# Attention pairs of a conv network: transposes re-ordered against scores and projection, 3x3 taps of two strips started earlier, one group norm of the next layer moved

## The chip, the core and the metric

The kernel runs on one core of one Trainium2 chip. A core has five engines that run side by side and wait for each other by semaphores: TensorE (PE in the profile: matmuls and, with an identity as one operand, transposes), VectorE (DVE), ScalarE (ACT), GpSimd (POOL) and SyncE (SP, which here issues the DMAs). Each engine takes its own instructions in the order in which the program has written them. The metric is the device time in microseconds of the whole launch, four images long; the median of three runs is the number that counts. Beside it there is one execution under the hardware profiler, whose span and instructions are what the profile shows.

## The reference, cut to what matters

Four images of 256 channels by 64 by 64 pass through four pre-normed layers. The change touches the first two, which are the same function with different weights:

```python
def layer(x):                       # layers 0 and 1, x: (b, 256, 64, 64)
    xn = group_norm(x)              # each pair of columns by its mean and variance over channels, rows
    y  = mhsa(xn)                   # tanh/sigmoid gates, a scan along the image: gives y
    q, k, v = split(windows(y) @ qkv_w.T + qkv_b)       # 64 windows of 8 x 8 tokens
    idx = top_k(mean(q) @ mean(k).T, 4)                 # routing: 4 windows for each window
    kg, vg = k[idx], v[idx]                             # gather: 256 keys and values
    a   = softmax(q * SCALE @ kg.T) per head            # 8 heads of 32 channels
    out = a @ vg
    out = out + depthwise_conv3x3(v_img, lepe_w) + lepe_b
    return x + out @ wo_w.T + wo_b
```

The work is cut into eight strips of 8 columns of the image; a strip holds four of the norm's groups, so its statistics need that strip only. Layers 2 and 3 are state-space layers, which the change leaves alone.

## The kernel before, in words

The four images are processed one after the other by unrolled code; each goes through attention layer 0, attention layer 1 and then the two state-space layers. An attention layer has three stages.

**Scan stage** (`scan_phase`). Eight strips. For strip s it computes the gates, the scan, and, one strip late, `keys_values(s - 1)`: the V and K projections on PE, V written by ACT into the image buffer `vimg` (L357), a copy on POOL into window order (`vst`, L361), eight transposes into `vt`, copies `vn` by DVE and ACT (L389, L390) and the DMAs of K and V to DRAM. The 3x3 depthwise convolution ("taps", made by `lepe`) of strip s - 3 is done on DVE between these. `lepe(lay, s, ...)` returns the steps of strip s: for each half m of the channels nine taps. On DVE a tap is one instruction (`step`); on POOL the first is one and every other is two (`weigh` into the one buffer `tap`, then `add` into `vimg`), so that a half is 9 steps on DVE and 17 on POOL. `[:9]` is half 0 with DVE's steps, `[17:]` half 1 with POOL's. The buffer of `weigh` has the tag `sq`, one buffer, which the squares of the group norm (`gn_sq`) share.

**Routing stage** (`routing`, and the lines after it in `attention_layers`). The means, the logits, the top four; then the queries of strips 2 to 4, with nine DVE taps between them and 17 POOL taps behind them, both of strip 5.

**Window stage** (`window_phase`). 32 iterations of one pair of windows each, i = 4 sj + a. The heads are cut in two parities, h = 0 and 1. For each pair and parity:

- `scores(i, h)`: 32 small matmuls into `sc`, one buffer for each parity; needs the gathered keys and the exponentials of the previous pair out of that buffer.
- `smallest(i, h)`: the reduction `mn` on DVE (L550).
- `exps(i, h, part)`: four exponentials on ACT (L561), in two parts.
- `normalise(i, h)`: the reciprocal `sm` on DVE (L573) and four multiplications of `pr` on POOL (L576).
- `turn(i, h)`: eight transposes on PE (L589) into two buffers `pt`, which both parities share.
- `turned(h, j)`: the copies `pts` out of `pt`, j = 0 by DVE (L600), j = 1 by ACT (L602).
- `values(i)`: 64 small matmuls (L615), once for each pair; `own_rows(i)` (L626) adds them into `vimg`.

Beside these an iteration may hold one convolution on PE (L232): `project(sj - 1, a - 1)` for a = 1, 2 (output projection; its result is added to `x` by DVE at L636, the call `add()` at the end of the iteration) and the late queries of strips 6 and 7 for a = 3 and a = 0 from i = 19 on (their result is written by ACT, `evict()`, also at the end). These convolutions and the small statistic matmuls of the norms share one PSUM buffer, tag `mm`. POOL taps of strip 6 (half 1) and strip 7 (both halves) are put two to an iteration, one behind each `normalise`; DVE taps of strip 6 (half 0) one to an iteration from i = 2 to 10. Group norms of the next layer's strips 0 and 1 (layer 0), or the statistics for layer 2 (layer 1), are put into iterations by `plan`: a list `mids`, run ahead of `normalise(i, 0)`, and a list `ends`, run at the end of the iteration. A norm has seven steps: sums (DVE), a matmul for the mean, center (DVE copy and a POOL subtraction, L151), square (ACT, L156), reduce (DVE), a matmul for the variance, scale (POOL power L168 and multiplication L172).

The order of work is written out by hand; nothing reorders it. Thus the order on PE around the change is, before, for an iteration with a convolution: scores(i, 1), turn(i-1, 1), convolution, scores(i+1, 0), values(i-1), turn(i, 0), the statistic matmul if there is one, scores(i+1, 1), and so on.

Of the kernel before, what the change touches and what calls it, by code (L numbers as in the profile page):

```python
# [23 lines left out]
NW = 8  # L24
# [20 lines left out]
class Net:  # L45
# [33 lines left out]
    def attention_layers(self, x, w_drams, v_drams):  # L79
        tc, nc = self.tc, self.nc  # L80
        with ExitStack() as ctx:
# [235 lines left out]
            def scan_phase(lay, work, psum, tail):  # L317
# [78 lines left out]
                for s in range(NW):  # L396
                    g = gn_four(lay, s + 2, lambda: psum) if s + 2 < NW else [lambda: None] * 4
                    taps = lepe(lay, s - 3, psum) if s >= 3 else []
                    g[0]()
                    xn = lay["xn"].pop(s).rearrange("p c w h -> p c (w h)")  # L400
                    ha, ha_half = hidden("ha", W1A, xn, AF.Tanh, vec[:, B1A : B1A + 2])
                    hb, hb_half = hidden("hb", W1B, xn, AF.Tanh, vec[:, B1B : B1B + 2])
                    z, z_half = hidden("z", W2A, ha, AF.Tanh, vec[:, B2A : B2A + 2])

                    f, f_half = hidden("f", W2B, hb, AF.Tanh, lay["half_b2b"], scale=0.5)
                    for half in (ha_half, hb_half):
                        half(0)
                        half(1)
                    for t in taps[:9]:
                        t()  # L410
                    if s == 0:
                        for t in tail:
                            t()
                        load_attention_weights(lay)
                    g[1]()
                    z_half(0)
                    z_half(1)
                    for t in taps[9:]:
                        t()
                    g[2]()  # L420
                    f_half(0)
                    f_half(1)
                    scan(s, f, z)
                    if s:
                        keys_values(s - 1)
                    g[3]()
                    if s >= 6:
                        double(s - 6)
                    if s in (5, 6):
                        for evict in [query(lay, s - 5, m, psum) for m in range(2)]:  # L430
                            evict()
                keys_values(NW - 1)


            def routing(lay, work, psum):
# [30 lines left out]

            def window_phase(lay, work, psum, idx, nxt):
                vec, wb = lay["vec"], lay["wb"]  # L470
                n_pair = NW * NW // 2
                regs, kv, pr, sm, ov = {}, {}, {}, {}, {}
# [125 lines left out]
                def turned(h, j):  # L598
                    if j == 0:
                        nc.vector.tensor_copy(pts[h][0], pt[h][0])  # L600
                    else:
                        nc.scalar.activation(pts[h][1], pt[h][1], AF.Copy)  # L602
# [47 lines left out]
                early = [query(lay, 5, m, psum, nc.vector, tag="pt", bufs=2) for m in range(2)]  # L650
                smallest(0, 0)
                smallest(0, 1)
                taps6, taps7 = (lepe(lay, s, pool=True) for s in (NW - 2, NW - 1))
                taps = taps6[17:] + taps7[17:] + taps7[:17]
                dve_taps = lepe(lay, NW - 2)[:9]

                mids, ends, left = {}, {}, []

                def plan(steps, *where):
                    for f, (at, i) in zip(steps, where):  # L660
                        if i < n_pair:
                            at.setdefault(i, []).append(f)
                        else:
                            left.append(f)

                if nxt:
                    load_scan_weights(nxt)
                    for s in range(2):
                        i = 10 + s
                        plan(gn(nxt, s, lambda: psum), (ends, i), (ends, i + 1), (mids, i + 2),  # L670
                             (ends, i + 2), (mids, i + 3), (ends, i + 5), (mids, i + 6))
                else:

                    for s in range(NW - 1):
                        i = 4 * s + 6
                        last = i + 6 if s < 5 else i + 3
                        plan(stats(s, lambda: psum), (ends, i), (ends, i + 1), (mids, i + 2),
                             (ends, i + 2), (ends, last), (mids, last + 1))
                for i in range(n_pair):
                    sj, a = divmod(i, 4)  # L680
                    add = evict = None
                    exps(i, 0, (0, 1))
                    if i:
                        scores(i, 1)
                        turned(0, 0)
                        turned(0, 1)
                        turn(i - 1, 1)
                        smallest(i, 1)
                    exps(i, 0, (2, 3))
                    for t in mids.get(i, ()):  # L690
                        t()
                    if i == 0:
                        for f in early:
                            f()
                    normalise(i, 0)
                    for t in taps[2 * i : 2 * i + 1]:
                        t()
                    if a == 3 and sj + 2 in (NW - 2, NW - 1):
                        evict = query(lay, sj + 2, 0, psum)
                    elif a == 0 and sj + 1 in (NW - 2, NW - 1):  # L700
                        evict = query(lay, sj + 1, 1, psum)
                    elif a in (1, 2) and sj:
                        add = project(sj - 1, a - 1, psum)
                    exps(i, 1, (0, 1))
                    scores(i + 1, 0)
                    if i:
                        turned(1, 0)
                        turned(1, 1)
                        values(i - 1)
                    turn(i, 0)  # L710
                    smallest(i + 1, 0)
                    exps(i, 1, (2, 3))
                    normalise(i, 1)
                    if i:
                        own_rows(i - 1)
                    for t in taps[2 * i + 1 : 2 * i + 2]:
                        t()
                    for t in dve_taps[i - 2 : i - 1] if i > 1 else ():
                        t()
                    if add:  # L720
                        add()
                    if evict:
                        evict()
                    gather(i + 3)
                    if a == 0 and 1 < sj + 1 < NW - 2:
                        double(sj + 1)
                    elif a == 1 and sj + 1 in (NW - 2, NW - 1):
                        double(sj + 1)
                    indices(i + 4)
                    for t in ends.get(i, ()):  # L730
                        t()
                turned(0, 0)
                turned(0, 1)
                turn(n_pair - 1, 1)
                turned(1, 0)
                turned(1, 1)
                values(n_pair - 1)

                def tail(m):
# [17 lines left out]
            for i, lay in enumerate(layers):  # L757
                with tc.tile_pool(name=f"at_a{i}", bufs=1, reuse_waits="tile") as work, tc.tile_pool(
                    name=f"at_p{i}", bufs=5, space=PSUM, reuse_waits="tile"
                ) as psum:  # L760
                    box["psum"] = psum
                    scan_phase(lay, work, psum, tail)
                    idx = routing(lay, work, psum)
                    taps = lepe(lay, NW - 3, psum)[:9]
                    for s in range(2, 5):
                        evicts = [query(lay, s, m, psum, nc.vector) for m in range(2)]
                        for t in taps[3 * s - 6 : 3 * s - 3]:
                            t()
                        for evict in evicts:
                            evict()  # L770
                    for t in lepe(lay, NW - 3, pool=True)[17:]:
                        t()
                with tc.tile_pool(name=f"at_c{i}", bufs=1, reuse_waits="tile") as work, tc.tile_pool(
                    name=f"at_q{i}", bufs=1, space=PSUM, reuse_waits="tile"
                ) as psum:
                    nxt = layers[i + 1] if i + 1 < len(layers) else None
                    box, tail, left = window_phase(lay, work, psum, idx, nxt)
                    if nxt is None:
                        box["psum"] = psum
                        g = stats(NW - 1, lambda: psum)  # L780
                        for t in (left[0], tail[0], left[1], tail[1], g[0], left[2], left[3], *g[1:]):
                            t()
# [1381 lines left out]
```

## Time and profile before

| | us |
|---|---|
| median of three runs | 12000.62 (11998.52 to 12002.84) |
| the profiled execution, its own time | 11985.03 |
| its span, first to last instruction | 11983.3 |
| PE busy over the span | 10083.2 (84%) |
| DVE busy | 9833.8 (82%) |
| POOL busy | 8811.5 (74%) |
| ACT busy | 7002.3 (58%) |

An image takes about 2990 us of this. In the first image the window stage of layer 0 lies from 233 to 484 us and that of layer 1 from 700 to 951 us, counted from the first `mn` to the last; there are eight such stretches in the launch, each 248 to 253 us long and 2009.0 us together. The rest of an image is the scan stages and the state-space layers.

Busy time alone says little here: in the window stages all four engines hand work to each other in short pieces. The useful views are the timeline of one engine at a time, in which each line gives the start, the length, what it is, and in square brackets how long the engine sat idle before it and what released it; and the table of stretches with busy time and the clock that PE was granted (1.00 is full speed).

### The profile page before, as it was taken

How to read it: one execution, taken by the hardware profiler on the slowest of the kernel's cores; microseconds unless marked ns; L12 is line 12 of the kernel's file. 1: busy time of each engine (PE TensorE's matmuls, PEld its weight loads, DVE VectorE, ACT ScalarE, POOL GpSimd, SP SyncE). 2: the span in 40 equal slices, each digit the busy share in tenths (PEclk: the TensorE clock that was granted, in tenths of full speed). 3: DMA queues.
4: the chain of work that ended last, by engine and by line, in shares of the span. 5: the costliest groups of instructions: out<-in, count | busy, mean ns of one | idle time of the engine just before them, and what ended most of it. 6: DMA issues, size and time to landing. Idle time of an engine off the chain costs nothing.

```text
span 11983.3 us, 192241 instructions
## 1 busy us (share of the span) xinstructions
PE 10083.2 (84%) x71104; PEld 5778.2 (48%) x71104; DVE 9833.8 (82%) x8350; ACT 7002.3 (58%) x13096; POOL 8811.5 (74%) x6054
## 2 busy tenths in 40 slices
PE   8998887777899888777799988877778998887777
PEld 4564554444455455444445645544444554554444
DVE  6677998998666799899866779989986667998998
ACT  4555555776455555477645555547764555554776
POOL 4666886898456688689745668868984666887897
PEclk9999998999999899899999989989999999998999
DMA  3343454454334355445433434444543343454454
GB/s 96 100 126 134 174 175 149 169 180 160 92 98 127 134 173 177 145 169 182 159 90 99 128 132 173 174 148 167 180 160 91 100 127 135 173 176 146 169 176 154
DMA packets 682506, 1742.10 MB, mean 145 GB/s; under 512 B 88896, under 2 KB 194896, under 8 KB 681312
## 3 DMA queue, kind: packets, MB, share of 16 engines
q1 hardware_dynamic: 676448, 1721.41, 43.1%
q10 hardware_dynamic: 5120, 8.39, 0.3%
q8 instruction: 563, 9.22, 0.3%
q14 instruction: 375, 3.07, 0.1%
HBM read 1601.52 MB, written 94.39 MB: 142 GB/s over the span
## 4 chain that ended last, share of the span: by engine, by line
DVE 23%; PE 23%; ACT 8%; issue 5%; POOL 4%; DMA 1%; SPq 0%; DVEq 0%; POOLq 0%; ACTq 0%
DVE h L1002 13%; DVE pb L996 5%; PE conv_ps L232 4%; PE y L954 4%; PE u_ps L1291 3%; ACT da L938 2%; PE pb L926 1%; PE u_ps L1664 1%; POOL pr L576 1%; PE sc L538 1%; DVE lp L270 1%; PE pt_ps L589 1%; ACT dap L938 1%; PE z_ps L1316 1%; POOL hc L1008 1%
## 5 line engine op out<-in xcount | busy, mean ns | idle before, releaser
L1008 POOL TENSOR_TENSOR hc<-h,cb 128x1024 f32<-128x1024 f32 x2056 | 4809.6, 2350 | 806.4 <-DVE h L1002 350.9
L1002 DVE TENSOR_TENSOR_SCAN h<-da,m_state,pb 128x1024 f32<-128x1024 f32 x1248 | 2920.6, 2340 | 161.4 <-DVE pb L996 2.4
L954 PE MATMUL y<-ident,hc 128*128 128x128 f32 x16384 | 2333.6, 290 | 408.0 <-POOL hc L1008 340.9
L954 PEld LDWEIGHTS y<-ident,hc 128*128 128x128 f32 x16384 | 2034.5, 150 | 1124.9 <-POOL hc L1008 577.0
L996 DVE TENSOR_TENSOR pb<-du,pb 128x1024 f32<-128x1024 f32 x1672 | 2025.4, 1211 | 113.4 <-PE pb L926 110.9
L938 ACT ACTIVATE da<-delta,m_v 128x1024 f32<-128x1024 f32 x1672 | 1899.5, 1141 | 135.5 <-DVE h L1002 118.3
L926 PE MATMUL pb<-m_parts,pick 128*128 128x512 bf16 x3312 | 1078.2, 410 | 846.1 <-DVE h L1002 777.6
L576 POOL TENSOR_SCALAR pr<-pr,sm,zero 128x256 f32<-128x256 f32 x2048 | 1136.5, 569 | 476.8 <-DVE sm L573 475.8
L561 ACT ACTIVATE pr<-sc,mn 128x256 f32<-128x256 f32 x2048 | 955.9, 482 | 647.5 <-DVE sm L573 480.9
L926 PEld LDWEIGHTS <-pick 128*128 128x128 bf16 x3312 | 263.1, 101 | 1787.4 <-DVE h L1002 981.2
L550 DVE TENSOR_REDUCE mn<-sc 128x4 f32<-128x1024 f32 x512 | 627.9, 1228 | 550.0 <-PE sc L538 547.2
L1002 DVE TENSOR_TENSOR_SCAN h<-da,pb 128x1024 f32<-128x1024 f32 x424 | 969.5, 2287 | 55.1 <-DVE pb L996 0.9
L912 POOL TENSOR_TENSOR bb<-du,bb 128x1024 f32<-128x1024 f32 x376 | 888.6, 2363 | 88.8 <-DMA bb<-m_cd 84.0
L589 PE MATMUL pt_ps<-ident,pr 128*128 128x128 f32 x4096 | 705.4, 304 | 144.3 <-POOL pr L576 51.1
L1002 DVE TENSOR_TENSOR_SCAN h<-dap,m_state,bb 128x1024 f32<-128x1024 f32 x288 | 672.4, 2335 | 65.1 <-ACT dap L938 45.9
L232 PE MATMUL conv_ps<-att_y,att_wb 128*128 128x512 f32 x1536 | 683.3, 594 | 1.3 <-DVE gn_mean L206 1.3
L589 PEld LDWEIGHTS pt_ps<-ident,pr 128*128 128x128 f32 x4096 | 490.3, 151 | 307.5 <-POOL pr L576 161.7
L538 PE MATMUL sc<-kv,q_swap 32*64 32x128 f32 x8192 | 597.2, 287 | 6.7 <-DMA kv<-kv_dram 4.7
L938 ACT ACTIVATE dap<-delta,m_v 128x1024 f32<-128x1024 f32 x376 | 419.7, 1116 | 304.0 <-DVE h L1002 234.2
L538 PE MATMUL sc<-kv,att_y 32*64 32x128 f32 x7168 | 569.2, 287 | 11.8 <-DMA kv<-kv_dram 7.5
L538 PEld LDWEIGHTS sc<-kv,att_y 32*64 32x64 f32 x7168 | 430.0, 139 | 144.9 <-ACT pr L561 65.6
L270 DVE SCALAR_TENSOR_TENSOR lp<-vimg,att_v,lp 128x512 f32<-128x512 f32 x616 | 465.4, 756 | 28.1 <-DVE lp L270 1.4
(300 smaller groups left out, 17937.9 us busy)
## 6 DMA issues: line engine op xcount, KB each, us to landing
cb<-m_cd SPq DMA_DIRECT2D x2048, 512.0 KB, 3.8
kv<-kv_dram SPq DMA_DIRECT2D x1984, 128.0 KB, 2.8
bb<-m_cd SPq DMA_DIRECT2D x376, 512.0 KB, 5.4
kv_dram<-kst SPq DMA_DIRECT2D x128, 256.0 KB
kv_dram<-vn SPq DMA_DIRECT2D x128, 256.0 KB, 4.1
q_swap<-att_y SPq DMA_DIRECT2D x96, 256.0 KB, 4.3
m_pe<-in_pe_dram SPq DMA_DIRECT2D x32, 512.0 KB, 4.1
out_dram<-yo SPq DMA_DIRECT2D x64, 256.0 KB, 2.4
```

The costliest lines, as they stand in the source:

```text
L232: nc.tensor.matmul(ps, w[:, k, w0 + m * P : w0 + (m + 1) * P], src[:, k], start=(k == 0), stop=(k == 1),)
L538: nc.tensor.matmul(sc[h][b * 64 : b * 64 + 64, r, w, m, :], (own(sj, m) if r == b else swap[sj % 2][:, m])[rows, 2 * a + w], kv[i, w][rows ...
L561: nc.scalar.activation(t[:, g].rearrange("p j r t -> p r j t"), sc[h][:, :, g // 2, g % 2, :].rearrange("p r (j t) -> p r j t", j=2), AF.E ...
L576: nc.gpsimd.tensor_scalar(t[:, g], t[:, g], s[:, g : g + 1], self.zero, ALU.mult, ALU.add)
L589: nc.tensor.transpose(pt[h][j][:, g, :], t[:, g, j].rearrange("p r t -> p (r t)"), self.ident,)
L912: nc.gpsimd.tensor_tensor(pb[i], slots[i][0]["du"], pb[i], ALU.mult)
L926: nc.tensor.matmul(pb[i][:, ss], self.pick[:, n : n + 1].to_broadcast([P, P]), blk["parts"][:, ss], start=True, stop=True,)
L938: nc.scalar.activation(da[i], blk["delta"], AF.Exp, scale=blk["a"](n))
L954: nc.tensor.matmul(blk["y"][:, ss], t[:, ss], self.ident, is_transpose=True, start=(n == 0 and ss.start % NT == 0), stop=(n == DS - 1 and ...
L996: nc.vector.tensor_tensor(pb[i], blk["du"], pb[i], ALU.mult)
L1002: nc.vector.tensor_tensor_scan(h[i][:, ss], da[i][:, ss], pb[i][:, ss], state, ALU.mult, ALU.add)
L1008: nc.gpsimd.tensor_tensor(hc[i][:, ss], h[i][:, ss], cb[i][:, ss], ALU.mult)
```

## The change

1. In the scan stage, before and around the last `keys_values`, the taps of strip 5 are done: nine on DVE, 17 on POOL, five of these ahead of `keys_values(7)` and twelve behind it.
2. In the routing stage the DVE taps are now those of strip 6 (nine), and the first nine POOL steps of strip 6 follow; the other eight go into the window stage.
3. In the window stage POOL has one tap step in an iteration in place of two, behind `normalise(i, 1)`: the eight left of strip 6 and 17 of strip 7. Half 0 of strip 7 goes to DVE, in the places where half 0 of strip 6 was. So POOL does 25 tap steps there in place of 51.
4. `turn(i, 0)` is written at the start of iteration i + 1, ahead of `scores(i+1, 1)`, and `turn(i, 1)` behind that iteration's convolution, ahead of `scores(i+2, 0)`.
5. The second norm of the next layer is spread over iterations 14 to 28 in place of 11 to 17.

On the engines the order comes out so. PE, with a convolution: scores(i, 1), convolution, turn(i-1, 1), scores(i+1, 0), values(i-1), the statistic matmul if there is one, turn(i, 0), scores(i+1, 1). So the convolution and turn(i-1, 1) change places, the statistic matmul goes ahead of turn(i, 0), and in iterations without either the order is as it was. ACT's order differs only in the place of the second norm's square; SP's and its DMAs' not at all; DVE has eight more groups of nine taps in the whole launch, each ahead of the last `vn`, and the moved steps of the norm.

```diff
@@ scan_phase
                         for evict in [query(lay, s - 5, m, psum) for m in range(2)]:
                             evict()
+                for t in lepe(lay, NW - 3, psum)[:9]:
+                    t()
+                later = lepe(lay, NW - 3, pool=True)[17:]
+                for t in later[:5]:
+                    t()
                 keys_values(NW - 1)
+                for t in later[5:]:
+                    t()
@@ window_phase
-                taps6, taps7 = (lepe(lay, s, pool=True) for s in (NW - 2, NW - 1))
-                taps = taps6[17:] + taps7[17:] + taps7[:17]
-                dve_taps = lepe(lay, NW - 2)[:9]
+                taps = taps + lepe(lay, NW - 1, pool=True)[17:]
+                dve_taps = lepe(lay, NW - 1)[:9]
...
-                    for s in range(2):
-                        i = 10 + s
-                        plan(gn(nxt, s, lambda: psum), (ends, i), (ends, i + 1), (mids, i + 2),
-                             (ends, i + 2), (mids, i + 3), (ends, i + 5), (mids, i + 6))
+                    plan(gn(nxt, 0, lambda: psum), (ends, 10), (ends, 11), (mids, 12),
+                         (ends, 12), (mids, 13), (ends, 15), (mids, 16))
+                    plan(gn(nxt, 1, lambda: psum), (ends, 14), (ends, 16), (mids, 17),
+                         (ends, 18), (mids, 19), (ends, 27), (mids, 28))
...
                     if i:
+                        turn(i - 1, 0)
                         scores(i, 1)
                         turned(0, 0)
                         turned(0, 1)
-                        turn(i - 1, 1)
                         smallest(i, 1)
...
                     normalise(i, 0)
-                    for t in taps[2 * i : 2 * i + 1]:
-                        t()
...
                     exps(i, 1, (0, 1))
+                    if i:
+                        turn(i - 1, 1)
                     scores(i + 1, 0)
                     if i:
                         turned(1, 0)
                         turned(1, 1)
                         values(i - 1)
-                    turn(i, 0)
                     smallest(i + 1, 0)
                     exps(i, 1, (2, 3))
                     normalise(i, 1)
                     if i:
                         own_rows(i - 1)
-                    for t in taps[2 * i + 1 : 2 * i + 2]:
+                    for t in taps[i : i + 1]:
                         t()
@@ attention_layers
-                    taps = lepe(lay, NW - 3, psum)[:9]
+                    taps = lepe(lay, NW - 2, psum)[:9]
...
-                    for t in lepe(lay, NW - 3, pool=True)[17:]:
+                    later = lepe(lay, NW - 2, pool=True)[17:]
+                    for t in later[:9]:
                         t()
```

## The prediction, made before the changed kernel ran

> **What bounds the kernel now.** I read the table of stretches first, to see where the engines are least full, then the group list of the page, then the timelines of single engines in the window stage, where all but the taps of the change happen. Two window stages, layer 0 and layer 1 of the first image (columns: us, busy us and count of PE, weight loads, DVE, ACT, POOL, then the granted PE clock, DMA share, GB/s):
>
> ```profile
> 233.30:484.29 250.99, 227.12 (x4502) 164.45 (x4491) 161.23 (x249) 155.69 (x570) 197.09 (x305) 0.92 0.49 147
> 699.95:950.92 250.97, 228.11 (x4520) 167.82 (x4512) 166.13 (x261) 170.48 (x617) 185.66 (x300) 0.91 0.49 143
> ```
>
> PE is the fullest, but its clock averages 0.92 and 0.91, and part of "busy" is matmuls at half speed. From starts at full clock in the timeline I take PE's needs: scores 1.03 us a parity, transposes 1.02 a parity, values 1.03, a convolution 1.81. A pair without convolution needs 2 x 1.03 + 2 x 1.02 + 1.03 = 5.13, with one 6.94. From the first `mn` to the last there are 31 pairs and 18 convolutions (14 projections, 4 queries): 31 x 5.13 + 18 x 1.81 = 191.6. The eight stretches take 2009.0, so 2009.0 - 8 x 191.6 = 476 us are waits and slow clock. Next, what PE and POOL wait for:
>
> ```profile
> L576 POOL TENSOR_SCALAR pr<-pr,sm,zero 128x256 f32<-128x256 f32 x2048 | 1136.5, 569 | 476.8 <-DVE sm L573 475.8
> ...
> L589 PE MATMUL pt_ps<-ident,pr 128*128 128x128 f32 x4096 | 705.4, 304 | 144.3 <-POOL pr L576 51.1
> ```
>
> POOL idles 476.8 us ahead of `normalise` for reciprocals, some 60 in each stage: it is seldom the bound, whatever its tap load. The transposes are where PE waits (144.3). The timeline of pair 6, layer 0 (DVE, POOL, PE), shows why:
>
> ```profile
> 279.75 1.22 DVE L550 TENSOR_REDUCE mn<-sc 128x4 f32<-128x1024 f32 x1 [2.53 <-PE sc L538]
> 280.89 0.17 DVE L573 RECIPROCAL sm<-sm 128x4 f32<-128x4 f32 x1
> ...
> 282.18 1.35 DVE L636 SCALAR_TENSOR_TENSOR x<-conv_ps,att_v,x 128x512 f32<-128x512 f32 x1
> ...
> 281.16 2.59 POOL L576 TENSOR_SCALAR pr<-pr,sm,zero 128x256 f32<-128x256 f32 x4 [1.01 <-DVE sm L573]
> ...
> 283.81 1.03 PE L589 MATMUL pt_ps<-ident,pr 128*128 128x128 f32 x5 [0.21 <-POOL pr L576]
> 284.67 1.88 PE L232 MATMUL conv_ps<-vimg,att_wb 128*128 128x512 f32 x4
> ```
>
> It is a ring: scores(6,0) end, mn, reciprocal, `normalise(5,1)`, turn(5,1), convolution, scores(7,0): 279.75 to the next `mn` at 287.66, 7.9 us. PE stands at turn(5,1) with the convolution, which needs nothing of it, behind.
>
> Two other places are dear. In layer 0 the square of the next norm sits in ACT's queue until POOL has finished a tap (its buffer is the taps'):
>
> ```profile
> 339.07 1.19 POOL L256 TENSOR_TENSOR vimg<-vimg,tap 128x512 f32<-128x512 f32 x1
> ...
> 340.29 1.06 ACT L156 ACTIVATE gn_sq<-att_xn 128x1024 f32<-128x1024 f32 x1 [6.34 <-POOL vimg L256]
> ...
> 352.39 1.06 ACT L156 ACTIVATE gn_sq<-att_xn 128x1024 f32<-128x1024 f32 x1 [6.43 <-POOL vimg L256]
> ```
>
> Pairs 13, 14 and 17 of layer 0 last 15.4, 12.4 and 13.7 us (distance of `mn` lines). In layer 1 ACT's four squares stand ahead of a copy for which turn waits, and then PE runs slow (conv 3.36, not 1.88):
>
> ```profile
> 806.14 0.91 PE L589 MATMUL pt_ps<-ident,pr 128*128 128x128 f32 x4 [1.17 <-ACT pts L602]
> 806.84 3.36 PE L232 MATMUL conv_ps<-vimg,att_wb 128*128 128x512 f32 x4
> ```
>
> **What the Trainium skill says.** "TensorE: Matmul & The Clock Gate", Part 1 (the clock gate): PE falls to half rate after an idle window of about 3.4 us and needs a busy one to recover. The trace agrees in kind: the stretch 332.27 to 347.63 was granted 0.67 and its transposes and convolution take double; so a wait taken away is worth more than itself. "GPSIMD Engine Reference", 1. Specifications: POOL's memory ports are shared with VectorE's two-input operations. It agrees: `normalise` is 2.16 us alone and 2.59 beside L270 and L636. "Perfetto Trace Analysis", Per-engine timelines: ACT, DVE and POOL are strict FIFO. It agrees: exponentials stand behind `gn_sq` above.
>
> **The change part by part.**
>
> *Taps ahead of the routing.* DVE gets nine (0.8 + 8 x 0.775 = 7.0 us) ahead of the last `vn`, which before waits idle:
>
> ```profile
> 217.81 0.69 DVE L389 COPY vn<-vt_ps 128x512 f32<-128x512 f32 x1 [7.10 <-PE vt_ps L383]
> ...
> 212.99 0.67 POOL L361 COPY vst<-vimg 128x512 f32<-128x512 f32 x1 [5.12 <-ACT vimg L357]
> ```
>
> 7.0 in a hole of 7.1, and POOL's five steps (0.75 + 2 x 2.13 = 5.0) in one of 5.12. Behind the last `vst` POOL has 12 + 9 steps: 6 x 2.13 + 0.75 + 4 x 2.13 = 22.1, so from 215.3 to 237.4, and the first `normalise` starts at 238.37. Behind `vn` are the DMAs of V and then the gathers; a slip of 0.3 us costs 0.3. Cost: 0, between 0 and 1 us a stage.
>
> *Half the taps out of the window stage.* 26 steps of about 0.97 = 25 us of POOL a stage. PE's path got POOL late only in pairs 1 to 4, where taps run between two `normalise` (in the stretch 238.49 to 245.34, pair 1 of layer 0, POOL was busy for 6.85 of 6.85 us). Layer 0's pairs 1 to 3 end at the gather of pair 3, for which PE waits 2.07 us; nothing is won there. Gain 1 us in a layer-1 stage, 0 in layer 0; between 0 and 4.
>
> *turn(i-1, 1) behind the convolution.* The 1.81 us run while POOL normalises. PE then has 6.94 in place of 7.2 (steady pairs 20 to 26 of layer 0), 7.9 or 8.4. But the convolution needs `mm`, freed by `add()` of the iteration before. In pair 6 that DVE work ends at 283.5, 3.75 after `mn`; PE is ready for the convolution 3.08 - 0.17 = 2.9 after `mn`. It waits 1.0, and pair 6 stays at about 7.85. Pairs 5, 9, 13 and 17 follow a pair without `add()`: gains of 1.0, 0.8 to 1.5, and where turn waits for ACT (13, 17, 29 of layer 1) the convolution fills the wait and keeps the clock: 2.9, 2.2, 2.5. Copies of turn(i-1, 1) now have only scores(i+1, 0), 1.03, to hide in before values(i-1): DVE needs 0.69 and ACT 0.6 plus hand-over; no-conv pairs live with that today and pay 0 to 0.62. I take 0.
>
> *Statistic matmuls ahead of turn(i, 0).* Each needs `mm`. In layer 1 iterations 19, 20, 23, 24 (query written by ACT) I count 0.9 us each; in 29 `add()` ends 2.1 later than PE comes, against 1.02 seen before.
>
> *Second norm.* Layer 0 loses the square at 352.39 and its subtraction: pairs 12 to 14 gain 0.5 + 3.0 + 5.2. The same square returns in pair 19 (parts: wait for `normalise(18,1)` and the tap add, 2.16 + 1.19, then 1.06; the convolution fills 1.8; loss 2.6), the sums in pair 15 (a DVE step of 1.22: loss 1.3), the scale in pair 28: 1.65 + 1.90 ahead of `normalise(28,0)`, PE idle about 3, then half clock: loss 4.5. Pairs 17, 18: 0.5 + 0.7 gained, since the subtraction (2.47) replaces the scale (3.55).
>
> **Sum.** Layer 0: gains 5: 1.0, 8 and 11: 0.5, 9: 0.8, 12 to 14: 8.7, 17 and 18: 1.2, 20 to 26: 1.4, 30: 0.2, together 13.8; losses 1.3 + 2.6 + 4.5 = 8.4; net -5.4. Layer 1: gains 1 to 4: 1.0, 5: 1.0, 9: 1.5, 8, 10 and 12: 1.0, 13: 2.9, 17: 2.2, 14, 18, 22 and 26: 1.2, 19 and 23 (where the wait for `pts`, 0.85, goes): 1.8, 29: 2.5, together 15.1; losses 20, 21, 24, 25: 0.6, 30: 0.5; net -14.0. An image -19.4; I add -2.6 for a warmer clock in pairs not listed (an estimate: 0.01 of clock over the 250 us of one of the two stages). -22 x 4 = -88. The profiled execution would come to 11985.0 - 88 = 11897; the median lies 15.6 above it, so 12000.6 - 88 = 11912.6, rounded 11912. The bounds: with every doubtful term at its good end (norm moved for free, no wait for `mm`) layer 0 gives -16 and layer 1 -24, four times 40 is -160: 11841; at the bad end +3 and -4: 11997.
>
> **Rivals.**
> - *The clock stays full.* Fewer waits could keep PE warm through most of a stage: clock 0.91 to 0.97 saves 251 x 0.06 = 15 us more in each of eight, -208: 11793. For it: 20 to 26 at 1.00. Against: the starts of both stages and the norm's waits keep cooling it. Chance 0.16.
> - *The fill is hidden anyway.* POOL's idle time says that its relief is worth nothing, and the wait for `add()` eats what the convolution gives, in most pairs as in pair 6: the layer-1 gains of 13, 17 and 29 alone, half kept: -15 in all: 11986. Chance 0.10.
> - *Slower: the norm's split cools PE twice more.* One mechanism: each lone wait of some 3 us in the window stage of layer 0 (square in 19, scale in 28) halves the clock for a window and costs 7 where I put 2.6 and 4.5, while pairs 13 and 14 do not mend since the first square still waits for POOL (saving 3, not 8.7). Layer 0 then reads -5.4 + 4.4 + 2.5 + 5.7 = +7.2, and if the statistic matmuls stall layer 1 as much as its turns gain, the launch is +29: 12029. With layer 1 at zero and a saving of 3, it decides once the losses at 19 and 28 together pass 7 us. Chance 0.10.
> - The forecast, with its spread: 0.64.
>
> **How the numbers follow.** About 24 us (0.2%) is what can be told from no change. Of the forecast's 0.64 some 0.02 lies inside that; with the second rival (half inside): faster 0.83, same 0.07, slower 0.10. The range, 11815 to 11992, covers the forecast's bounds, the near half of the first rival and the second.
>
> **What would show it.** After: convolutions begin at the end of scores(i, 1); layer 0's pairs 20 to 26 near 6.95; pair 14 near 7.2; pairs 19 and 29 of layer 0 longer; `vn` with hardly any idle before it; waits of the mean and variance matmuls in layer 1 for x or ACT. Wrong: if stages keep 250 us, or `vn` waits for nothing and the first scores come later.

## The result, and the profile after

| | before | after |
|---|---|---|
| median of five runs, us | 12000.62 (11995.56 to 12006.89) | 12054.64 (12046.58 to 12063.26) |
| ratio, 95% interval | | 1.0046 (1.0031 to 1.0060) |
| profiled execution, us | 11985.03 | 12063.26 |
| first `mn` to last, four stages of layer 0 | 1000.4 | 1015.3 |
| the same, four stages of layer 1 | 1008.6 | 1045.2 |

The changed kernel is 54 us slower where 88 us less were forecast. The eight window stages grew by 51.6 us, so the loss lies there. (The profiled executions differ by 78; the other 27 lie outside the window stages. Before's profiled execution is 15.6 us below its own median. Outside the stages it took 9974 us, and the executions of the later kernels scatter there over 9983 to 10012 us, so I explain only the 51.6.)

The page of the changed kernel, three of its groups (from the scores on, L538 before, the line numbers of the changed kernel are 7 higher; above they are the same):

```profile
L583 POOL TENSOR_SCALAR pr<-pr,sm,zero 128x256 f32<-128x256 f32 x2048 | 1142.9, 575 | 667.2 <-DVE sm L580 666.3
...
L596 PE MATMUL pt_ps<-ident,pr 128*128 128x128 f32 x4096 | 662.3, 304 | 79.5 <-POOL pr L583 33.1
...
L232 PE MATMUL conv_ps<-att_y,att_wb 128*128 128x512 f32 x1536 | 690.1, 599 | 11.3 <-DVE gn_mean L206 11.3
```

The aim of the new order was reached: PE waits 79.5 us ahead of the transposes where it waited 144.3. POOL, with fewer taps, only idles longer (667.2 where it was 476.8). The third line is the clue: convolutions waited 11.3 us in the launch for a tiny DVE copy of group-norm statistics, 1.3 us before. (It has only the convolutions of one input; the whole comes below.) The table of stretches for the two window stages of the first image, changed kernel, with the columns of the prediction's first fence:

```profile
232.98:489.72 256.74, 232.11 (x4503) 171.75 (x4491) 162.53 (x249) 157.48 (x570) 177.52 (x283) 0.89 0.51 144
705.02:969.12 264.10, 236.37 (x4520) 177.36 (x4512) 167.51 (x260) 173.10 (x617) 166.07 (x278) 0.86 0.47 135
```

Layer 1 was 250.97 us at a clock of 0.91 and is 264.10 at 0.86. So PE waits for something and, being colder, also works slower. The waits of PE in that layer-1 stage name it (waiting line, what for, us in total, times, longest). Three lines of before that the prediction did not look at:

```profile
PE gn_pv L195 <- DVE x L636: 1.0, 1, 1.0
PE conv_ps L232 <- DVE gvar L221: 0.4, 1, 0.4
PE conv_ps L232 <- DVE gn_mean L206: 0.3, 2, 0.2
```

and of the changed kernel:

```profile
PE conv_ps L232 <- DVE gvar L221: 8.5, 6, 1.4
PE pt_ps L596 <- DVE pts L607: 4.2, 4, 1.3
PE conv_ps L232 <- DVE gn_mean L206: 2.8, 2, 1.4
PE ov_ps L622 <- ACT pts L609: 2.8, 6, 0.6
PE gn_pv L195 <- DVE x L643: 2.0, 1, 2.0
...
PE pt_ps L596 <- POOL pr L583: 1.8, 7, 0.6
PE gn_pm L195 <- ACT q_late L298: 0.7, 2, 0.5
```

Eight convolutions of the stage wait 1.4 us each, 11.3 us together, for the copies `gvar` and `gn_mean`; before they waited 0.7 us in all. Why 1.4 us each time, the timeline around iteration 29 of layer 1 shows (DVE, then PE; in brackets the idle time ahead and who ended it):

```profile
943.77 1.23 DVE L557 TENSOR_REDUCE mn<-sc 128x4 f32<-128x1024 f32 x1 [2.11 <-PE sc L545]
944.91 0.15 DVE L221 COPY gvar<-gn_pv 128x4 f32<-128x4 f32 x1
...
952.71 1.30 DVE L643 SCALAR_TENSOR_TENSOR x<-conv_ps,att_v,x 128x512 f32<-128x512 f32 x1
```

```profile
945.12 3.78 PE L232 MATMUL conv_ps<-vimg,att_wb 128*128 128x512 f32 x4 [1.42 <-DVE gvar L221]
...
954.16 0.36 PE L195 MATMUL gn_pv<-gn_s,one_gn 128*128 128x4 f32 x2 [2.03 <-DVE x L643]
```

The last score matmul ends at 943.71. The convolution is next on PE and needs the one buffer `mm`, which still holds the variance that an earlier statistic matmul wrote. The copy that empties it is in `mids(i)`, and on DVE `mids(i)` stands behind `smallest(i, 1)`: DVE first waits for the scores, reduces them for 1.23 us, and only then copies for 0.15. In the kernel before, turn(i-1, 1) stood between scores(i, 1) and the convolution and covered these 1.4 us. The second PE line is the mirror image: the statistic matmul, now ahead of turn(i, 0), takes `mm` from a convolution whose result DVE has not yet added to `x`, and the transposes that need nothing of it stand behind.

The convolution takes 3.78 us here. In iteration 20, after a wait just as long, it took 1.98:

```profile
865.84 1.98 PE L232 MATMUL conv_ps<-att_y,att_wb 128*128 128x512 f32 x4 [1.42 <-DVE gn_mean L206]
```

The table of stretches shows that the wait is not what first slowed it. PE had half speed (0.50) already ahead of the wait of iteration 29, and full speed around that of iteration 20:

```profile
926.00:943.70 17.70, 17.70 (x284) 14.98 (x276) 7.57 (x15) 12.71 (x44) 8.71 (x16) 0.50 0.50 146
864.00:874.00 10.00, 7.69 (x166) 5.54 (x158) 5.03 (x9) 7.23 (x24) 5.72 (x10) 1.00 0.48 140
```

Of the eight waits for copies in this stage, two are followed at once by a stretch at 0.50 (809.43 to 812.84 and 908.42 to 911.83), four by full speed, and two come while PE is at half speed already. So the waits are sure; that each of them cools PE is not.

### The profile page after: what moved, and what is told of

The parts are those of the page before. It is cut to its first block, busy times and chain, and to the rows that moved or that the text cites. A ratio compares the mean times of both kernels' runs of the same rounds, so it can differ in the third digit from the quotient of the medians.

```text
span 12061.5 us, 191725 instructions
## 1 busy us (share of the span) xinstructions
PE 10131.8 (84%) x70632; PEld 5859.0 (49%) x71104; DVE 9899.0 (82%) x8422; ACT 7019.9 (58%) x13096; POOL 8706.7 (72%) x5918
## 5 line engine op out<-in xcount | busy, mean ns | idle before, releaser
L931 PE MATMUL pb<-m_parts,pick 128*128 128x512 bf16 x2840 | 971.9, 413 | 837.1 <-DVE h L1007 771.4
L583 POOL TENSOR_SCALAR pr<-pr,sm,zero 128x256 f32<-128x256 f32 x2048 | 1142.9, 575 | 667.2 <-DVE sm L580 666.3
L596 PE MATMUL pt_ps<-ident,pr 128*128 128x128 f32 x4096 | 662.3, 304 | 79.5 <-POOL pr L583 33.1
L232 PE MATMUL conv_ps<-att_y,att_wb 128*128 128x512 f32 x1536 | 690.1, 599 | 11.3 <-DVE gn_mean L206 11.3
L596 PEld LDWEIGHTS pt_ps<-ident,pr 128*128 128x128 f32 x4096 | 522.7, 157 | 257.3 <-POOL pr L583 106.6
L545 PE MATMUL sc<-kv,q_swap 32*64 32x128 f32 x8192 | 621.4, 294 | 13.9 <-DMA q_swap<-q_late 8.4
L607 DVE COPY pts<-pt_ps 128x512 f32<-128x512 f32 x512 | 353.0, 689 | 293.7 <-PE pt_ps L596 292.8
L270 DVE SCALAR_TENSOR_TENSOR lp<-vimg,att_v,lp 128x512 f32<-128x512 f32 x672 | 507.7, 756 | 31.2 <-DVE lp L270 1.4
```

The costliest lines, as they stand in the source:

```text
L232: nc.tensor.matmul(ps, w[:, k, w0 + m * P : w0 + (m + 1) * P], src[:, k], start=(k == 0), stop=(k == 1),)
L545: nc.tensor.matmul(sc[h][b * 64 : b * 64 + 64, r, w, m, :], (own(sj, m) if r == b else swap[sj % 2][:, m])[rows, 2 * a + w], kv[i, w][rows ...
L583: nc.gpsimd.tensor_scalar(t[:, g], t[:, g], s[:, g : g + 1], self.zero, ALU.mult, ALU.add)
L596: nc.tensor.transpose(pt[h][j][:, g, :], t[:, g, j].rearrange("p r t -> p (r t)"), self.ident,)
L931: nc.tensor.matmul(pb[i][:, ss], self.pick[:, n : n + 1].to_broadcast([P, P]), blk["parts"][:, ss], start=True, stop=True,)
```

## The experiments

The theory (S where the expectations use a letter), from these lines: the loss is the shared buffer `mm`, in two forms: the convolution waits for a copy that stands late in DVE's queue, and the statistic matmul waits for the result of a convolution. Rivals: the split of the second norm (the forecast's own slower case), and the taps moved ahead of the routing. All kernels were timed in five rounds beside the kernel before, whose median was 12010.32 beside a_turns to n_cols, 12007.79 beside o_both to p_both_tap and 12003.98 beside the last two of the table; so ratios are compared. Stage sums are of one profiled execution each. How far they scatter is seen from o_both and q_both_nonorm, which have the same code in layer 1: 946.4 and 959.1.

| kernel | median us | ratio to before (95%) | layer 0, four stages | layer 1, four stages |
|---|---|---|---|---|
| after | 12054.64 | 1.0046 (1.0031 to 1.0060) | 1015.3 | 1045.2 |
| a_turns | 12057.40 | 1.0037 (1.0024 to 1.0049) | 995.2 | 1056.8 |
| b_noturns | 12013.67 | 1.0003 (0.9995 to 1.0011) | 1016.0 | 1004.8 |
| m_mids | 11958.08 | 0.9960 (0.9948 to 0.9972) | 957.6 | 977.5 |
| n_cols | 12017.96 | 1.0004 (0.9996 to 1.0013) | 1013.2 | 1008.5 |
| o_both | 11917.21 | 0.9924 (0.9911 to 0.9938) | 974.7 | 946.4 |
| r_both_b | 11936.46 | 0.9938 (0.9925 to 0.9952) | 971.2 | 974.5 |
| q_both_nonorm | 11920.25 | 0.9928 (0.9915 to 0.9942) | 975.6 | 959.1 |
| p_both_tap | 11882.62 | 0.9898 (0.9883 to 0.9913) | 943.0 | 950.7 |
| l_b_tap | 11969.75 | 0.9973 (0.9962 to 0.9984) | 966.3 | 1012.3 |
| s_tap_nonorm | 11869.21 | 0.9886 (0.9871 to 0.9901) | 925.2 | 959.9 |

**Which part loses: a_turns and b_noturns.** The first is the kernel before with the new places of the transposes alone; the second is the changed kernel with the old places.

```diff
 a_turns, against before
                     if i:
+                        turn(i - 1, 0)
                         scores(i, 1)
                         turned(0, 0)
                         turned(0, 1)
-                        turn(i - 1, 1)
                         smallest(i, 1)
...
                     exps(i, 1, (0, 1))
+                    if i:
+                        turn(i - 1, 1)
                     scores(i + 1, 0)
...
-                    turn(i, 0)
```

> The kernel before with the new places of the transposes alone; taps and norm as before. Theory S (the one statistic and convolution buffer: with the convolution directly behind scores(i,1), it waits 1.4 us for a DVE copy of the statistics that stands behind mn(i,1), in eight iterations of a layer-1 stage, and the statistic matmul ahead of turn(i,0) waits up to 2 us; each also cools PE): slower than before, 12020 to 12050, layer-1 stages near 260 us. Theory N (the norm's split and the moved taps cost the time, the transposes gain): not slower than before, 11930 to 12000, layer-1 stages below 250.

> The changed kernel with the transposes put back to their old places; taps and second norm as changed. Theory S: the loss goes, 11970 to 12005, layer-1 stages at 250 or a little under. Theory N: the loss stays or grows, 12050 to 12100, in the layer-0 stages.

The transposes alone give 1.0037, the whole change without them 1.0003. (Both medians lie some 8 us above the range given for S, far from those for N.) The loss of the launch is theirs. It is in layer 1 (+48 us over the four stages, layer 0 -5), and there the waits of a_turns are those of the changed kernel (first image; L636 is L643 there):

```profile
PE conv_ps L232 <- DVE gvar L221: 8.5, 6, 1.4
...
PE conv_ps L232 <- DVE gn_mean L206: 2.8, 2, 1.4
PE gn_pv L195 <- DVE x L636: 2.0, 1, 2.0
...
PE gn_pm L195 <- ACT q_late L298: 1.0, 2, 0.5
```

Taps and norm together give nothing that can be measured in the launch; in the profile layer 0 of b_noturns is 16 us longer and layer 1 4 us shorter. The changed kernel's layer 0, 15 us longer, is thus more like b_noturns than like a_turns: that part goes with taps and norm, if it is more than scatter.

**Which wait loses: m_mids and n_cols.** Both are the changed kernel. m_mids runs the list `mids` ahead of `smallest(i, 1)`, so that the copy out of `mm` stands before the reduction on DVE. In layer 1 the list holds such copies alone. In layer 0 the norm's subtraction, reduction and scaling stand in it too and move along. n_cols puts turn(i, 0) back ahead of the statistic matmul.

```diff
 m_mids, against after
                         turned(0, 0)
                         turned(0, 1)
+                        for t in mids.get(i, ()):
+                            t()
                         smallest(i, 1)
                     exps(i, 0, (2, 3))
-                    for t in mids.get(i, ()):
-                        t()
```

```diff
 n_cols, against after
                     if i:
-                        turn(i - 1, 0)
                         scores(i, 1)
...
                     indices(i + 4)
+                    turn(i, 0)
                     for t in ends.get(i, ()):
                         t()
                 for h in range(2):
-                    turn(n_pair - 1, h)
+                    if h:
+                        turn(n_pair - 1, h)
```

> The changed kernel with the list of mid-iteration steps run ahead of smallest(i,1) in place of behind it, so that the copy of the statistics frees the buffer before the convolution comes. Theory S: the waits of the convolution for gn_mean and gvar (11.3 us and the like in the changed kernel) vanish; 8 of 1.4 us in a layer-1 stage and the cooling that follows: 11 to 20 us a stage less, 11970 to 12010. Theory N: no change, within 10 us of 12055.

> The changed kernel with turn(i,0) written ahead of the statistic matmul again (turn(i-1,1) stays behind the convolution). Theory S: takes the wait of about 2 us in iteration 29 and those of up to 0.5 us elsewhere, about 4 us a layer-1 stage: 12030 to 12045; the convolution's waits for the copies stay. Theory N: no change, within 10 us of 12055.

PE's waits in layer 1 of the first image of m_mids: no convolution waits for a copy any more, and the statistic matmuls wait as before this edit.

```profile
PE gn_pv L195 <- DVE x L643: 1.9, 1, 1.9
...
PE gn_pm L195 <- ACT q_late L298: 1.0, 2, 0.5
...
PE conv_ps L232 <- DVE x L643: 0.5, 1, 0.5
```

And of n_cols: the convolutions wait as long as in the changed kernel, while the wait of `gn_pm` is gone and that of `gn_pv` is down from 2.0 to 0.8.

```profile
PE conv_ps L232 <- DVE gvar L221: 8.5, 6, 1.4
...
PE conv_ps L232 <- DVE gn_mean L206: 2.8, 2, 1.4
...
PE gn_pv L195 <- DVE x L643: 0.8, 1, 0.8
```

Each edit takes away its own wait and leaves the other. From the changed kernel's ratio of 1.0046, m_mids takes 0.0086 and n_cols 0.0042, both more than was expected. In layer 1 the four stages lose 67.7 us by m_mids and 36.6 by n_cols. So both waits cost there, the copy's about twice as much.

The other 57.7 us of m_mids are in layer 0, where only one convolution a stage waited for a copy, 1.4 us. There the late copy holds up POOL as well. In iteration 28 of the changed kernel (first two lines) the DVE step of the norm's scaling stands behind `mn`; POOL idles 3.04 us, then does the scaling, and `normalise` waits behind it. In m_mids (last two lines) the step comes ahead of `mn`, and POOL scales in the time in which it had idled:

```profile
463.58 0.15 DVE L167 TENSOR_SCALAR gn_rstd<-gn_pv 128x8 f32<-128x8 f32 x1
463.82 1.65 POOL L168 TENSOR_TENSOR gn_rstd<-gn_rstd,minus_half 128x8 f32<-128x8 f32 x1 [3.04 <-DVE sm L580]
...
444.18 0.15 DVE L167 TENSOR_SCALAR gn_rstd<-gn_pv 128x8 f32<-128x8 f32 x1
444.42 1.65 POOL L168 TENSOR_TENSOR gn_rstd<-gn_rstd,minus_half 128x8 f32<-128x8 f32 x1
```

Ahead of the four such POOL steps (L151, L168) of the first layer-0 stage POOL idled 8.1 us in the changed kernel, 4.6 in the kernel before and not at all in m_mids. So part of what m_mids gives is no repair: the kernel before could have had it. The edit was not run on that kernel, and in layer 0 no run separates POOL's wait from that of the convolution.

**Both mends: o_both.** m_mids and n_cols in one kernel.

> The changed kernel with both mends: the mid-iteration steps ahead of smallest(i,1), and turn(i,0) ahead of the statistic matmul. If the two waits are separate, their savings add: 12055 - 96 - 40 = 11920, 11905 to 11935. If they are one loss by way of the clock (either mend keeps PE warm enough), no better than the mid-iteration mend alone: 11945 to 11965.

0.9924, which is 0.0122 below the changed kernel; the two savings add (0.0086 + 0.0042 = 0.0128). At 11917 us it stands where the change itself was forecast, with a help that the forecast did not count (POOL's earlier norm steps). Its two stages in the table of stretches:

```profile
232.13:472.77 240.64, 222.64 (x4503) 166.66 (x4491) 162.61 (x250) 157.88 (x570) 177.61 (x284) 0.91 0.54 153
688.22:924.23 236.01, 220.47 (x4520) 168.82 (x4512) 167.41 (x261) 171.80 (x617) 166.06 (x278) 0.93 0.54 152
```

The same place of layer 1, DVE and then PE: the copy of 0.15 us is done before the scores end, and the convolution follows them without a wait.

```profile
906.17 0.15 DVE L221 COPY gvar<-gn_pv 128x4 f32<-128x4 f32 x1
907.18 1.23 DVE L557 TENSOR_REDUCE mn<-sc 128x4 f32<-128x1024 f32 x1 [0.86 <-PE sc L545]
```

```profile
907.04 1.99 PE L232 MATMUL conv_ps<-vimg,att_wb 128*128 128x512 f32 x4
```

**What the other parts are worth once the waits are mended: r_both_b and q_both_nonorm.** r_both_b is a_turns with both mends (taps and norm as before). q_both_nonorm is o_both with the second norm at iterations 11 to 17, close to its old place:

```diff
-                    plan(gn(nxt, 1, lambda: psum), (ends, 14), (ends, 16), (mids, 17),
-                         (ends, 18), (mids, 19), (ends, 27), (mids, 28))
+                    plan(gn(nxt, 1, lambda: psum), (ends, 11), (ends, 12), (mids, 13),
+                         (ends, 14), (mids, 15), (ends, 16), (mids, 17))
```

> The kernel before with the new places of the transposes and both mends, taps and norm left as before. If POOL's lighter load and the norm's split are worth nothing, as my rival said, this equals the kernel with everything and both mends within 15 us. If they are worth something once the transposes no longer bind, it is slower than that kernel by 20 us or more.

> The changed kernel with both mends and the second norm put back near its old places (sums at 11, square at 14, scale at 17). If spreading the norm costs (my loss of 8.4 against a gain of 10 in a layer-0 stage), it is within 10 us of the kernel with both mends; if the slower rival was right that each lone wait cools PE, 15 to 40 us faster than that one; if the spreading pays, 15 us slower or more.

Once both waits are mended the norm's place makes no difference that can be measured (0.9928 and 0.9924). The split exists in layer 0 alone, and most of the loss is in layer 1. So the rival of the split falls as the main cause. The changed kernel with the old norm and without the mends was not run. r_both_b is 19 us above o_both, but the intervals touch, so whether taps and norm together are worth anything here is not settled.

**The buffer that taps and squares share: p_both_tap, l_b_tap, s_tap_nonorm.** In the changed kernel the squares of the norms still wait for POOL's taps. The timeline of ACT in layer 0, changed kernel:

```profile
334.61 1.06 ACT L156 ACTIVATE gn_sq<-att_xn 128x1024 f32<-128x1024 f32 x1 [5.60 <-POOL vimg L256]
```

An own buffer for the taps takes that wait away. The same edit was made to o_both (p_both_tap), to the kernel before (l_b_tap) and to q_both_nonorm (s_tap_nonorm).

```diff
                     def weigh():
-                        both = norm.tile([P, 2, 8, S], F32, tag="sq", name="tap", bufs=1)
-                        box[m] = both[:, m]
+                        box[m] = norm.tile([P, 8, S], F32, tag="tap", name="tap", bufs=1)
```

> The changed kernel with both mends and a buffer of its own for the taps, so that the norm's square no longer waits for POOL. Two squares in a layer-0 stage idle ACT for 5.6 and 4.3 us in the changed kernel; if these waits are on the path, 4 to 8 us a stage: 16 to 32 us faster than the kernel with both mends. If POOL is late for the transposes anyway, the same within 8.

> The kernel before with a buffer of its own for the taps, nothing else. In its layer-0 stages ACT idled 6.3 and 6.4 us ahead of the two squares. If that wait was what made pairs 13 and 14 last 15.4 and 12.4 us, they fall to 8 to 10 and the launch by 25 to 45 us, to 0.996 to 0.998 of before. If PE stood there for POOL's subtraction and the transposes anyway, less than 10 us.

> The changed kernel with both mends, the taps' own buffer and the second norm near its old places. With the buffer apart the square waits for nothing of POOL's, so the place of the norm should matter only by the scale's 3.55 us: within 12 us of the kernel with both mends and the own buffer, and by rival 'lone waits cool PE' 12 to 25 us faster (one late scale less, in pair 28).

In l_b_tap ACT's two squares, which sat idle 6.34 and 6.43 us before, wait 0.15 and 1.32, and now for their own operand:

```profile
330.36 1.06 ACT L156 ACTIVATE gn_sq<-att_xn 128x1024 f32<-128x1024 f32 x1 [0.15 <-POOL att_xn L151]
...
341.06 1.06 ACT L156 ACTIVATE gn_sq<-att_xn 128x1024 f32<-128x1024 f32 x1 [1.32 <-POOL att_xn L151]
```

Layer 0 loses 34 us over four stages and layer 1, which has no such squares between taps, nothing (+4); the launch 0.27%, as expected, though not where it was expected: pair 14 fell from 12.4 to 7.2 us, pair 13 only from 15.4 to 14.7. On top of both mends the edit brings 0.9898, 35 us and a little more than expected. s_tap_nonorm is the fastest kernel run, 0.9886 (11869 us), and beats both kernels of this study. The 13 us between it and p_both_tap would fit the rival by which each lone wait cools PE (12 to 25), but the intervals overlap, so this stays open.

## Why the prediction was wrong

**The step that failed** is, in the part "*turn(i-1, 1) behind the convolution*", the sentence "But the convolution needs `mm`, freed by `add()` of the iteration before". The buffer was named, but only one of its last users was looked up. In the iterations with a statistic the last user is a DVE copy in `mids(i)`; its place in DVE's queue was never read, and its wait was put at nothing. In its place PE waits 11.3 us for copies in a layer-1 stage. They fall in the very iterations, 13, 17 and 29 among them, where the convolution was to fill a wait.

A second term was mis-sized: the losses of the statistic matmuls, "20, 21, 24, 25: 0.6, 30: 0.5", together 1.1 us a layer-1 stage. Their waits were foreseen, and rather too long (2.1 us in iteration 29 and 0.9 in four others; the trace has 2.0 and at most 0.5). Their price was not: n_cols, which shortens them, is 36.6 / 4 = 9.2 us faster in a layer-1 stage. In the changed kernel the clock of that stage fell from 0.91 to 0.86.

How far this goes. A layer-1 stage was forecast at -14.0 and came to (1045.2 - 1008.6) / 4 = +9.2, a miss of 23.2 us; a layer-0 stage was forecast at -5.4 and came to (1015.3 - 1000.4) / 4 = +3.7, a miss of 9.1; the warmer clock, -2.6 an image, did not come. The two mends take (1045.2 - 946.4) / 4 = 24.7 and (1015.3 - 974.7) / 4 = 10.2 us away again. What is left against before, -15.6 and -6.4, adds up to the -22 of the forecast. That is in part luck: in layer 0 the mends also give POOL an earlier start that no term of the sum stands for, and single terms are off both ways, as follows.

Point by point:

- *Taps ahead of the routing: cost 0.* Right. `vn`, which sat idle 7.10 us, follows the taps at once, and the first `mn` comes at 232.98 (before: 233.30). From the last `mn` of layer 0 to the first of layer 1 the four images took 861.6 us together (before: 863.1):

```profile
217.01 0.75 DVE L270 SCALAR_TENSOR_TENSOR vimg<-vimg,att_v,lp 128x512 f32<-128x512 f32 x1
217.74 0.69 DVE L389 COPY vn<-vt_ps 128x512 f32<-128x512 f32 x1
```

- *Half the taps out of the window stage: gain 1 us in layer 1, 0 in layer 0.* Not contradicted; b_noturns shows no gain.
- *turn(i-1, 1) behind the convolution.* Right where `mm` was free. In layer 0 of the first image pairs 21 to 26 last 6.9 to 7.0 (7.2 before, 6.94 forecast), pair 5 went from 8.9 to 7.1, and pair 6 stays at 7.8, as worked out. In layer 1 pairs 13 and 29 were to gain 2.9 and 2.5 from 11.2 each and came to 11.8 and 13.5; in o_both both are 8.2, a gain of 3.0.
- *Losses at 20, 21, 24, 25 and 30 of layer 1, 1.1 together.* These five went from 7.6, 7.8, 7.6, 7.7 and 8.9 to 9.8, 8.9, 8.9, 10.5 and 13.3, together 11.7 us longer (from unrounded times), with the waits for copies in it.
- *Pairs 12 to 14 of layer 0: gain 8.7.* In the first image they went from 35.3 to 31.9, a gain of 3.4, and in the fourth by 2.7, as the slower rival said; in the second and third they went from 35.4 to 26.9, a gain of 8.5. In all four the first square still waits 5.6 us for a tap (the fence above), so that wait alone does not decide it.
- *The square in pair 19: loss 2.6; the scale in pair 28: loss 4.5.* Pair 19 went from 7.2 to 9.5 (2.3) with pair 20 1.2 longer; pairs 28 and 29 from 14.4 to 22.2 (7.8). PE after the scale is slow, as the forecast said, though it had waited only 1.75 us at once and not about 3:

```profile
468.05 2.95 PE L596 MATMUL pt_ps<-ident,pr 128*128 128x128 f32 x8 [1.75 <-POOL pr L583]
```

- *Pairs 17 and 18 of layer 0: gain 1.2.* They lost 1.2: iteration 17 holds a `mids` list, and its convolution waits for the copy of the mean, 1.4 us, and runs at half speed.

```profile
373.54 3.78 PE L232 MATMUL conv_ps<-vimg,att_wb 128*128 128x512 f32 x4 [1.42 <-DVE gn_mean L149]
```

- *Not foreseen:* pair 27 of layer 0 took 10.5 us in the first image (7.5 before), with a score matmul waiting 2.06 us for the DMA of the late queries. It was 6.2 in another image, and no run isolated it.
- *`normalise` "2.59 beside L270 and L636".* Only L270 counts. Of the kernel before's single multiplications, the 120 that ran beside L636 alone took 0.556 us (median), those beside no DVE work 0.555. L636 reads one operand from PSUM.

The slower rival had the right sign and only part of the reason. It priced the square in 19 and the scale in 28 at 7 us each; the scale came to that, the square did not, and a layer-0 stage is 3.7 us longer where it said 7.2. Most of the loss lies in layer 1, which it named only as a condition, "if the statistic matmuls stall layer 1 as much as its turns gain". The copies and the statistic matmuls stalled it by more than that.

What stays open: how much of the loss is waiting and how much the colder clock was not separated by a run, nor was why PE stayed at half speed from 926 to 943.7 us without waiting. A second buffer for the statistics, the plainest test of the shared one, was not tried.

## What to carry to other kernels

Before an instruction is moved ahead in one engine's queue, list each buffer that it writes, the last reader of that buffer, and where that reader stands in its own engine's queue: a copy of 0.15 us can stand behind a wait and a reduction. What stood between the two places is cover for such a wait, and it is gone after the move. In this kernel the copies that free the shared buffer belong ahead of the long work in their queue; that one edit turned a loss of 0.46% into a gain of 0.40%, though part of this came from POOL's earlier start in layer 0.

## What was not expected of the hardware

In the layer-1 stage of the changed kernel PE never waited longer than 2.0 us at once, and yet its clock was 0.86. If it has only full and half speed, as in the stretches shown, that is about 74 of 264 us at half speed (2 x 0.14 x 264, an estimate), and about 33 of 236 in o_both at 0.93. From the one kernel to the other some 13 us of waits leave a layer-1 stage (11.3 + 0.7 + 1.2), and the stage is (1045.2 - 946.4) / 4 = 24.7 us shorter. The prediction held the idle window of about 3.4 us that the Trainium skill gives ("TensorE: Matmul & The Clock Gate", Part 1) for the thing to look for; no wait in this stage is that long. It also took from that page that PE needs a busy window to recover; from 926 to 943.7 us PE was busy for 17.70 of 17.70 us by the profile, which models the ends of matmuls, and still at 0.50. The same page, section "A second HAM failure mode: psum-queue depth-cycling", describes something nearer to these traces: short idles between groups of matmuls, from cycling through PSUM, make the clock swing between full and half. Here the clock swings so, with waits of 1.4 to 2.0 us, but no run shows that these alone bring it about. "Perfetto Trace Analysis", Optimizing Tensor Performance, Matmuls, asks that independent groups of matmuls rotate through different PSUM banks so that emptying one overlaps the next. The waits for `mm`, 1.4 us eight times a layer-1 stage, are what one shared buffer cost in the new order.

The first POOL tap ahead of the routing took 1.67 us in place of 0.77, beside a DVE scan with two inputs; it cost nothing there, since POOL had room.
